# Layer 0 of a four-layer network: steps of 32 queries and all keys, head mixing on sixteen 32x32 tiles, transposes and key sums on VectorE

## The chip, the cores and the metric

The kernel runs on one NeuronCore of a Trainium2 chip. The metric is device time in microseconds (us) of one execution; less is better. The engines named below are TensorE (PE; its weight loads are listed as PEld), VectorE (DVE), ScalarE (ACT), GpSimd (POOL) and SyncE (SP), which issues most DMAs. SBUF is the on-chip memory of 128 partitions; PSUM takes TensorE's results, in eight banks of 512 float32 numbers per partition.

## What is computed

All data is float32. The input x is (4, 512, 32, 32): 4 images of 512 channels and 1024 positions ("tokens"). Each of four layers reads x normalized over groups of 16 channels and adds its result to x. The change is in layer 0, an attention whose 8 heads of 64 channels are mixed before the softmax, and whose probabilities are normalized over each whole map:

```python
q = jnp.einsum('oc,bct->bot', w_q, xf).reshape(b, heads, hd, t)   # k, v alike
attn = jnp.einsum('bhdq,bhdT->bhqT', q, k) * scale
attn = jnp.einsum('gh,bhqT->bgqT', w_head, attn)       # head mixing
attn = jax.nn.softmax(attn, axis=-1)
mean = jnp.mean(attn, axis=(-2, -1), keepdims=True)
var = jnp.var(attn, axis=(-2, -1), keepdims=True)
attn = (attn - mean) / jnp.sqrt(var + EPS)
attn = attn * in_gamma[None, :, None, None] + in_beta[None, :, None, None]
out = jnp.einsum('bhqT,bhdT->bhqd', attn, v)
out = out.reshape(b, t, c)
out = out @ w_proj.T + b_proj
```

Since the softmax's rows sum to 1, the map's mean is 1/1024; its variance needs the sum of squares of the probabilities. Layer 1 is a small simulated circuit that yields one factor per channel, layer 2 an ordinary attention, layer 3 a read of the 8 best of 2048 memory rows per token.

## The kernel before

Everything is in `fast_net`. Channels lie on partitions (`KC` = 4 chunks of 128). Layer 0 goes image by image. The projections q, k (`project`, matmuls at L159), v (`project_tokens`, L172) and the output p (`put_out`) each take 64 matmul instructions of 512 columns; a float32 matmul is recorded as two instructions.

The attention of one image is cut into 32 units `UNITS0` of 128 queries (block `j`) by 256 keys (part `c`).

- `scores` (L343): 8 matmuls with 64 rows (one head's channels) by 128 columns (queries), for the 8 heads, into two PSUM tiles. DVE (L351) and ACT (L353) copy them to `ss`. Eight DMAs of 128 KB on SP (L357) put the rows into `s2`, so that the 8 heads of 16 queries lie on the 128 partitions.
- `mix` (L374): one matmul per 16 queries x 128 keys, with the data as the stationary operand and the 128x128 matrix `wmix` (scale times `w_head`, block by block) as the moving one. The result has keys on partitions; ACT takes the exponential (L378) into `places`, and its square (L390). DVE sums the exponentials over the parts of 128 keys (L397), POOL sums the squares (L402).
- `apply` (L416): v times the exponentials, `pv` of 64x128 per head, two heads side by side in the column halves of the array. After the last part of a block, `finish` sums the remaining 128 partitions with matmuls against ones (L438); ACT copies, DVE inverts (L449) and scales `pv` into `o` (L466), POOL squares the scale (L450, L451). Rows of the inverse go to `seen`, by which the program checks at its end that the range of float32 held.

`pin` keeps an engine's instructions in the order in which they are written, so PE's order is that of the loop: `scores` of a unit, `mix` of the unit two before, `apply` of the one three before. `prepare` (the next image's statistics on DVE, L274, and normalization on DVE, L287) and `gating` (layer 1 of the image before) are generators that give a piece per unit. At the end of an image come q of the next image, the last units, k, `instance_norm` (the scale and shift of `o` on DVE, L498), v, the first two units of scores, and p. The `circuit` constants (DVE, POOL) come after the first image's v. SP's queue holds, in order, the `ss` to `s2` copies, the weights (`load_w`, L200, two buffers, each queued after the projection that frees its place) and the next image's x. POOL's queue holds additions and the DMAs of `put_out` (L511, L515).

Layers 2 and 3 come after layer 0 has ended for all images. In layer 2 the output rows pass through three buffers `xr` (L832 load, L833 ACT, L835 DVE, L836 store).

Of the kernel before, what the change touches and what calls it, by code (L numbers as in the profile page):

```python
# [40 lines left out]
def fast_net(ctx: ExitStack, tc: tile.TileContext, a: dict, out: bass.AP, flag: bass.AP):  # L41
# [7 lines left out]
    ps_s = stage.enter_context(tc.tile_pool(name="ps_s", bufs=2, space=PSUM))  # L49
    ps_t = stage.enter_context(tc.tile_pool(name="ps_t", bufs=2, space=PSUM))  # L50
    ps_m = stage.enter_context(tc.tile_pool(name="ps_m", bufs=2, space=PSUM))
# [5 lines left out]
    def mm_tile(name):  # L57
        return ps_m.tile([P, NB], F32, tag="mm", name=name)

    def small_ps(name):  # L60
        return ps_t.tile([P, NB], F32, tag="tp", name=name)
# [22 lines left out]
    for i in range(P // NH):  # L84
# [21 lines left out]
    )  # L106


    NQ16 = P // NH
    wmix = const.tile([P, NH, NQ16], F32, tag="wmix", name="wmix")  # L110
    nc.gpsimd.memset(wmix, SCALE)
    nc.gpsimd.affine_select(
        out=wmix, in_=wmix, compare_op=ALU.is_ge, fill=0.0, base=0,
        pattern=[[0, NH], [-NH, NQ16]], channel_multiplier=1,
    )
    nc.gpsimd.affine_select(
        out=wmix, in_=wmix, compare_op=ALU.is_ge, fill=0.0, base=NH - 1,
        pattern=[[0, NH], [NH, NQ16]], channel_multiplier=-1,
    )

    seen = const.tile([P, NB], F32, tag="seen", name="seen")
# [31 lines left out]
    def project(w, src, name, evacuate, chunks=range(KC)):  # L153

        for m in chunks:
            ps = ps_s.tile([P, T], F32, tag="sc", name=f"{name}_{m}")
            for n in range(T // NB):
                for k in range(KC):
                    pin(nc.tensor.matmul(  # L159
                        ps[:, n * NB:(n + 1) * NB],  # L160
                        w[:, k, m * P:(m + 1) * P], src[:, k, n * NB:(n + 1) * NB],
                        start=(k == 0), stop=(k == KC - 1),
                    ))
            evacuate(m, ps)

    def project_tokens(w, src, name, evacuate):

        for t in range(0, TC, 2):
            ps = ps_s.tile([P, 2, C], F32, tag="sc", name=f"{name}_{t}")
            for i in range(2):  # L170
# [11 lines left out]
    TB = 2 * P  # L182
    UNITS0 = [(j, c) for j in range(TC) for c in range(T // TB)]
    vs_row = [dram.tile([1, C], F32, tag=f"vs_{b}", name=f"vs_{b}") for b in range(B)]

# [1574 lines left out]
```

## Time and profile before

| | us |
|---|---|
| median of 3 runs (3045.35 to 3047.05) | 3046.58 |
| the profiled execution | 3045.97 |
| its span, first to last instruction | 3044.2 |
| PE busy | 2938.4 |
| DVE busy | 1694.3 |
| POOL busy | 1379.2 |
| ACT busy | 1153.2 |
| layer 0's mixing matmuls (`mx`, L374) | 499.6 |
| layer 0's scores (`sc`, L343) | 259.1 |
| layer 0's values (`pv`, L416) | 251.8 |
| layer 0 to 2 border, by the last p of layer 0 | 1641 |

Layer 0 takes the first 1641 us of the span, layer 2 up to about 2568, layer 3 the rest. The page tells the clock granted to TensorE as `PEclk`. In a group's row stand the line, the engine, the operation, what it writes and reads with the shape (rows*columns of the array for matmuls), the count, the busy us and mean ns of one, and the idle time before it. Busy is the union of the group's intervals; since matmuls are pipelined, busy divided by the count is the pace, and the mean is longer. In the order of time a line has start, length, engine, line and what it is.

### The profile page before, as it was taken

To read this page: it belongs to the slowest core of one execution; us is meant where nothing else is said; L and a number is where in the kernel's file an instruction comes from. 1 tells how busy PE (TensorE), PEld (TensorE's weight loads), DVE (VectorE), ACT (ScalarE), POOL (GpSimd) and SP (SyncE) were. 2 spreads that over 40 slices of the span, in tenths; PEclk is the share of its full clock that TensorE was granted. 3 is DMA by queue.
4 is the path that set the end of the run, shared out by engine and by line. 5 is a ranking of instruction groups with operands and counts; after the bars stand their busy time and mean duration, and the time that the engine had idled before them with its cause. 6 is when DMAs were issued, how large, how long until landed. Compare 5 with 4: busy or idle time off the path is not lost.

```text
span 3044.2 us, 41932 instructions
## 1 busy us (share of the span) xinstructions
PE 2938.4 (97%) x16102; PEld 1681.0 (55%) x16102; DVE 1694.3 (56%) x1588; ACT 1153.2 (38%) x1480; POOL 1379.2 (45%) x1147
## 2 busy tenths in 40 slices
PE   7799999999999999999999999999999999999995
PEld 3488855888558885588853334334334334444442
DVE  1377823778237782368633452461471444878876
ACT  0266612666126661266612421530440351221211
POOL 2066622666226661266612630650460362665664
PEclk9899999999999999999999999999999999999997
DMA  2345405554055440554423002101200203676665
GB/s 80 110 129 137 126 28 147 150 135 126 28 151 151 129 126 28 151 154 129 123 87 111 1 14 93 32 1 69 71 1 28 97 1 107 181 216 207 190 187 146
DMA packets 238696, 318.03 MB, mean 104 GB/s; under 512 B 34701, under 2 KB 198541, under 8 KB 234010
## 3 DMA queue, kind: packets, MB, share of 16 engines
q1 hardware_dynamic: 207368, 231.05, 26.2%
q0 software_dynamic: 29696, 84.18, 9.2%
q8 instruction: 130, 2.13, 0.3%
q14 instruction: 76, 0.62, 0.1%
q10 hardware_dynamic: 1426, 0.05, 0.0%
HBM read 155.52 MB, written 25.17 MB: 59 GB/s over the span
## 4 chain that ended last, share of the span: by engine, by line
PE 87%; DVE 4%; POOL 3%; issue 3%; DMA 1%; ACT 1%; SPq 0%; DVEq 0%; ACTq 0%; POOLq 0%
PE mx L374 15%; PE at L879 14%; PE pv L416 8%; PE p L159 7%; PE k L159 7%; PE sc L343 7%; PE v L172 7%; PE q L159 7%; PE sc_c L760 5%; PE pv_c L792 5%; PE sum L438 2%; POOL ep_c L776 1%; PE rs_c L811 1%; DVE es_c L777 1%; ACT places L768 1%
## 5 line engine op out<-in xcount | busy, mean ns | idle before, releaser
L397 DVE TENSOR_REDUCE places<-places 128x1024 f32<-128x3072 f32 (+1 forms) x128 | 429.0, 3352 | 284.3 <-ACT places L378 282.8
L402 POOL TENSOR_TENSOR es<-es,e 128x1024 f32<-128x1024 f32 x192 | 455.2, 2371 | 228.2 <-ACT e L390 220.0
L374 PE MATMUL mx<-wmix,s 128*128 128x128 f32 x4096 | 499.6, 280 | 1.4 <-ACT places L378 1.1
L374 PEld LDWEIGHTS mx<-wmix,s 128*128 128x128 f32 x4096 | 475.0, 191 | 45.0 <-issue 41.3
L879 PE MATMUL at<-memT,xn_d 128*128 128x512 f32 x1024 | 445.0, 592 | 0.0
L896 POOL DMA_INDIRECT got<-in_mem,ix x256 | 278.2, 1087 | 211.1 <-issue 110.4
L768 ACT ACTIVATE places<-sc_c 128x1024 f32<-128x1024 f32 x256 | 248.2, 1021 | 315.8 <-PE sc_c L760 296.0
L378 ACT ACTIVATE places<-mx 128x512 f32<-128x512 f32 x512 | 305.7, 597 | 158.9 <-PE mx L374 151.3
L879 PEld LDWEIGHTS at<-memT,xn_d 128*128 128x128 f32 x1024 | 192.1, 190 | 230.9 <-issue 230.6
L776 POOL TENSOR_TENSOR ep_c<-places 128x1024 f32<-128x1024 f32 x96 | 234.9, 2448 | 155.5 <-ACT places L768 149.4
L343 PE MATMUL sc<-k,q 64*128 64x256 f32 x2048 | 259.1, 392 | 18.2 <-DVE ss L351 15.2
L777 DVE TENSOR_TENSOR es_c<-es_c,ep_c 128x1024 f32<-128x1024 f32 x96 | 151.9, 1582 | 212.2 <-POOL ep_c L776 212.0
L760 PE MATMUL sc_c<-q,k 64*128 64x512 f32 x1024 | 257.4, 621 | 5.3 <-ACT places L768 3.7
L390 ACT ACTIVATE e<-places 128x1024 f32<-128x1024 f32 x256 | 255.6, 1048 | 1.0 <-POOL es L402 1.0
L416 PE MATMUL pv<-places,v 128*64 128x128 f32 x4096 | 251.8, 276 | 0.0
L792 PE MATMUL pv_c<-places,v 128*64 128x512 f32 x1024 | 249.2, 607 | 2.0 <-ACT places L768 2.0
L353 ACT COPY ss<-sc 128x1024 f32<-128x1024 f32 x128 | 129.5, 1012 | 289.9 <-PE sc L343 269.5
L416 PEld LDWEIGHTS pv<-places,v 128*64 128x64 f32 x4096 | 220.9, 137 | 18.0 <-issue 3.0
L343 PEld LDWEIGHTS sc<-k,q 64*128 64x128 f32 x2048 | 188.6, 188 | 76.5 <-issue 36.5
L351 DVE COPY ss<-sc 128x1024 f32<-128x1024 f32 x128 | 156.0, 1220 | 48.0 <-PE sc L343 31.2
L760 PEld LDWEIGHTS sc_c<-q,k 64*128 64x128 f32 x1024 | 88.9, 187 | 156.4 <-issue 129.5
L402 POOL TENSOR_TENSOR es<-e,e 128x1024 f32<-128x1024 f32 x32 | 75.4, 2355 | 218.7 <-ACT e L390 218.7
(227 smaller groups left out, 3151.1 us busy)
## 6 DMA issues: line engine op xcount, KB each, us to landing
s<-ss SPq DMA_DIRECT2D x1024, 128.0 KB
xn<-in_x SPq DMA_DIRECT2D x16, 512.0 KB
xr<-in_x POOLq DMA_DIRECT2D x32, 256.0 KB, 3.3
x<-xr POOLq DMA_DIRECT2D x32, 256.0 KB, 2.5
xn_c<-x SPq DMA_DIRECT2D x16, 512.0 KB
xr_c<-x SPq DMA_DIRECT2D x32, 256.0 KB
x<-xr_c SPq DMA_DIRECT2D x32, 256.0 KB
xn_d<-x SPq DMA_DIRECT2D x16, 512.0 KB
```

Of the source, the lines that this page charges most:

```text
L159: pin(nc.tensor.matmul(ps[:, n * NB:(n + 1) * NB], w[:, k, m * P:(m + 1) * P], src[:, k, n * NB:(n + 1) * NB], start=(k == 0), stop=(k == ...
L343: pin(nc.tensor.matmul(sc[:, r, m, :], q[r * HD:(r + 1) * HD, 2 * i + m, j * P:(j + 1) * P], k_[r * HD:(r + 1) * HD, 2 * i + m, c * TB:(c ...
L374: pin(nc.tensor.matmul(mx[:, i], s2[:, half * (NB // P) + i, t * P:(t + 1) * P], wmix, start=True, stop=True,))
L378: pin(nc.scalar.activation(e[:, :, half * (NB // P):(half + 1) * (NB // P), :], mx.rearrange("p i g q -> p g i q"), AF.Exp,))
L397: pin(nc.vector.tensor_reduce(es, places[:, at + (c == 0):at + 3].rearrange("p t g q -> p g q t"), AX.X, ALU.add))
L402: pin(nc.gpsimd.tensor_add(es2, e2s[0] if (c, t) == (0, 1) else es2, e2))
L416: pin(nc.tensor.matmul(pv[r * HD:(r + 1) * HD, gp, :], I["v"][:, tt, g * HD:(g + 1) * HD], ev[:, g, :], start=(tt == 0 and gp == 0), stop= ...
L760: pin(nc.tensor.matmul(sc[:, r, :], I["k"][r * HD:(r + 1) * HD, m, t * P:(t + 1) * P], I["q"][r * HD:(r + 1) * HD, m, n * NB:(n + 1) * NB] ...
L768: nc.scalar.activation(e, sc, AF.Exp)
L792: pin(nc.tensor.matmul(pv[r * HD:(r + 1) * HD, :], I["v"][:, t, h * HD:(h + 1) * HD], e[:, r, :], start=(t == 0), stop=(t == TC - 1),))
L879: pin(nc.tensor.matmul(sc[:, n * NB:(n + 1) * NB], xn3[b][:, k, tt * P:(tt + 1) * P], memT[k][:, i0:i0 + NB], start=(k == 0), stop=(k == K ...
L896: pin(nc.gpsimd.indirect_dma_start(out=got[:, i, :], out_offset=None, in_=a["mem"], in_offset=bass.IndirectOffsetOnAxis(ap=ix[:, i:i + 1], ...
```

## The change

Layer 0's attention goes in 32 steps per image of 32 queries and all 1024 keys.

- Scores: for each half of the keys, 8 heads' matmuls of 64 rows x 32 columns, moving 512 keys each, into one pair of banks `sc`; ACT copies both halves. Sixteen DMAs of 64 KB put 8 heads x 4 queries on each quarter of 32 partitions of `s2`.
- `mix`: `wmix` (32 x 32) is now the stationary operand, for 16 tiles of the array: row group r holds 8 queries (2 x 4), column group t takes a quarter of the keys. The result has head and query on partitions; ACT takes the exponentials, 1024 per instruction, into `e`.
- `reduce`: DVE's `bn_stats` (eight of 256 elements a step) gives mean and squared deviations, from which the sums over keys of the exponentials and of their squares follow; two DVE transposes of 32x32 blocks put keys back on partitions, into `eT`.
- `apply` runs seven steps behind, two key parts a step. `sums` adds the parts with one matmul of 32 columns per 128 queries; the inverse goes through DRAM (`r_rows`) and comes back spread (`rb`), by DMAs on POOL's queue. `scale` (DVE) writes blocks of `o` to DRAM (`o_rows`), and `collect` reads them back.
- The projections are fills in the steps: v in steps 0 and 1, p of the image before in steps 2 to 5, the next q in steps 32 to 35, k after the last step. All layer 0 PSUM tiles are fixed (`sc`, `pt`, `mx0`, `mx1`).
- `prepare`'s normalization and `instance_norm`'s scaling move from DVE to POOL, the `vs` DMAs from SP to POOL. The circuit comes before the first k. Weights share three buffers with `ss` (`ws`), and the output buffers `xr` are two in layers 0 and 2. Layers 2 and 3 take their other buffers from `e` and `eT`; layer 2 loads its weights in one place (`load2`).

```diff
-    ps_s = stage.enter_context(tc.tile_pool(name="ps_s", bufs=2, space=PSUM))
-    ps_t = stage.enter_context(tc.tile_pool(name="ps_t", bufs=2, space=PSUM))
-    ps_m = stage.enter_context(tc.tile_pool(name="ps_m", bufs=2, space=PSUM))
+    ps_a = stage.enter_context(tc.tile_pool(name="ps_a", bufs=1, space=PSUM))
+    mx = ps_a.tile([P, 4, NB], F32, tag="mx", name="mx")
+    pairs = {at: ps_a.tile([P, 2, NB], F32, tag=at, name=at) for at in ("sc", "pt")}
+    pairs.update(mx0=mx[:, 0:2], mx1=mx[:, 2:4])
...
+    NS = 32
...
+    o_rows = [dram.tile([P, TC, NB], F32, tag=f"o_{b}", name=f"o_{b}") for b in range(B)]
+    r_rows = [dram.tile([NS, NS], F32, tag=f"r_{i}", name=f"r_{i}") for i in range(2)]
...
+    STEPS = T // NS
+    LAG = 7
+    NK = T // 4
...
+    e = apool.tile([P, 2, 2, 2, NK], F32, tag="e", name="e")
+    eT = apool.tile([P, 2, TC, NS, NS], F32, tag="eT", name="eT")
+    eT_flat = eT.rearrange("p a b k x -> p (a b k x)")
+    o_full = eT_flat[:, 2 * KC * T:3 * KC * T]
+    wp_full = eT_flat[:, 3 * KC * T:3 * KC * T + KC * C].rearrange("p (k c) -> p k c", k=KC)
...
+        w = apool.tile([P, KC, C], F32, tag="ws", bufs=3, name=name)
...
+            pin(nc.gpsimd.tensor_scalar(
...
+    def take_k(b, m, at):
+        I = img[b]
+        if m == 0:
+            I["k"] = big("k", f"k0_{b}")
+        project(I["w_k"], tokens(I["xn"]), m, at,
+                lambda ps: pin(nc.vector.tensor_copy(
+                    I["k"][:, m, :].rearrange("p (t b j) -> p t j b", t=4, j=NS),
+                    ps.rearrange("p (t j b) -> p t j b", t=4, j=NS))))
...
+        project_tokens(I["w_v"], lambda k, t: I["xn"][:, k, t::TC], i, at,
+                       lambda ps: pin(nc.scalar.copy(I["v"][:, 2 * i:2 * i + 2, :], ps)))
...
+    def sum_v(b):
...
+        pin(nc.vector.tensor_scalar_mul(row, vps[0:1, :], float(T)))
+        nc.gpsimd.dma_start(out=vs_row[b], in_=row)
...
+    def scores(b, s, n):
+        I = img[b]
...
+        if n == 0:
+            I["ss", s] = apool.tile([P, 2, T], F32, tag="ws", bufs=3, name=f"ss_{b}_{s}")
+        ss = I["ss", s]
+        sc = pairs["sc"]
+        for m in range(KC):
+            for r in range(2):
+                pin(nc.tensor.matmul(
+                    sc[m * NS:(m + 1) * NS, r, :],
+                    q[r * HD:(r + 1) * HD, m, s * NS:(s + 1) * NS],
+                    k_[r * HD:(r + 1) * HD, m, n * NB:(n + 1) * NB],
+                    start=True, stop=True,
...
+        pin(nc.scalar.copy(ss[:, :, n * NB:(n + 1) * NB], sc))
+        if n == 0:
+            return
+        s2 = I["s2", s] = apool.tile([P, 2, T], F32, tag="s2", bufs=2, name=f"s2_{b}_{s}")
+        del I["ss", s]
+        for m in range(KC):
+            for r in range(2):
+                for qq in range(2):
+                    at = m * NS + qq * (NS // 2)
+                    nc.sync.dma_start(
+                        out=s2[r * KC + m::NH, qq], in_=ss[at:at + NS // 2, r, :])
+    def mix(b, s):
+        s2 = img[b].pop(("s2", s))
+        for t in range(4):
+            for r in range(4):
+                pin(nc.tensor.matmul(
+                    mx[t * NS:(t + 1) * NS, r, :].rearrange("p (qq k) -> p qq k", qq=2),
+                    wmix[r * NS:(r + 1) * NS], s2[r * NS:(r + 1) * NS, :, t * NK:(t + 1) * NK],
+                    start=True, stop=True,
...
+    def exps(s, half):
+        pin(nc.scalar.activation(
+            e[:, half].rearrange("p r qq k -> p (r qq k)"), flat2(pairs[f"mx{half}"]), AF.Exp))
+    def reduce(b, s, half):
+        I = img[b]
+        j, i = divmod(s, 4)
+        if s % 4 == 0 and half == 0:
+            I["st", j] = apool.tile([P, 4, 4, 2, 6], F32, tag="st", bufs=2, name=f"st_{b}_{j}")
+        st = I["st", j]
+        for r in range(2):
+            for qq in range(2):
+                pin(nc.vector.bn_stats(st[:, i, 2 * half + r, qq, :], e[:, half, r, qq, :]))
+        pin(nc.vector.transpose(
+            eT[:, j % 2].rearrange("p b (qq i r) x -> p i r qq b x", qq=2, i=4)[
+                :, i, 2 * half:2 * half + 2],
+            e[:, half].rearrange("p r qq (b x) -> p r qq b x", x=NS),
+        ))
+    def apply(b, s):
...
+                        eT[:, j % 2, t, :, 4 * g:4 * g + 4],
...
+        s_ = small.tile([P, 2, 4, 4], F32, tag="sums", name=f"sums_{nm}")
+        order = "p qq i r -> p i r qq"
+        pin(nc.gpsimd.tensor_add(s_.rearrange(order), st[:, :, :, :, 1], st[:, :, :, :, 4]))
+        yield
+        ps = small_ps(f"sum_{nm}")[:, 0:NS]
+        pin(nc.tensor.matmul(
+            ps, same, s_.rearrange("p qq i r -> p (qq i r)"), start=True, stop=True))
+        ri = small.tile([P, NS], F32, tag="ri", name=f"ri_{nm}")
+        pin(nc.vector.reciprocal(ri, ps))
...
+        rows = r_rows[j % 2]
+        pin(nc.gpsimd.dma_start(out=rows, in_=ri[0:NS]))
+        pin(nc.gpsimd.tensor_scalar(ok[:, 0], ri, R_LO, None, ALU.is_ge))
+        pin(nc.gpsimd.tensor_scalar(ok[:, 1], ri, R_HI, None, ALU.is_le))
+        for i in range(2):
+            pin(nc.gpsimd.tensor_add(seen0, seen0, ok[:, i]))
+        rb = I["rb", j] = apool.tile([P, KC, P], F32, tag="rb", bufs=2, name=f"rb_{nm}")
+        for r in range(2):
+            pin(nc.gpsimd.dma_start(
+                out=rb[r * HD:(r + 1) * HD],
+                in_=rows.rearrange("(gp r x) y -> r gp (x y)", r=2, x=4)[r].partition_broadcast(HD),
+            ))
...
+    def scale(b, j):
+        I = img[b]
+        rb = I.pop(("rb", j)).rearrange("p gp (q qq x) -> p qq gp x q", q=4, qq=2)
+        pv = pairs["pt"][:, 0, :].rearrange("p (gp qq x q) -> p qq gp x q", gp=KC, qq=2, q=4)
+        o = apool.tile([P, KC, NH, NS // 2], F32, tag="o2", bufs=2, name=f"o_{b}_{j}")
+        o_v = o.rearrange("p kc (gp r) x -> p r gp x kc", r=2)
+        for r in range(2):
+            h = slice(r * HD, (r + 1) * HD)
+            for par in range(2):
+                pin(nc.vector.tensor_mul(
+                    o_v[par * HD:(par + 1) * HD, r], pv[h, par], rb[h, par]))
+        nc.sync.dma_start(
+            out=o_rows[b][:, j, :], in_=o.rearrange("p kc g x -> p (kc g x)"))
+    def collect(b):
+        nc.sync.dma_start(
+            out=o_full.rearrange("p (j x) -> p j x", j=TC), in_=o_rows[b])
+        nc.sync.dma_start(out=wp_full, in_=a["w_proj"])
...
+        o = o_full.rearrange("p (jk g x) -> p g jk x", g=NH, x=NS // 2)
...
+            pin(nc.gpsimd.tensor_scalar(
+                o[:, g], o[:, g], al[:, g:g + 1], bb[:, g:g + 1], ALU.mult, ALU.add))
...
+    def put_out(b, m, at):
...
-                xr = apool.tile([P, NB], F32, tag="xr", bufs=3, name=f"xr_{b}_{m}_{n}")
+                xr = apool.tile([P, NB], F32, tag="xr", bufs=2, name=f"xr_{b}_{m}_{n}")
...
+        project(wp_full, lambda k, n: o[:, k, 4 * n:4 * n + 4], m, at, add_out)
...
-                xr = apool.tile([P, NB], F32, tag="xr", bufs=3, name=f"xr_c{b}_{m}_{n}")
+                xr = apool.tile([P, NB], F32, tag="xr", bufs=2, name=f"xr_c{b}_{m}_{n}")
...
     first()
-    take_k(0)
-    take_v(0)
     circuit()
...
+    for m, at in enumerate(("mx1", "sc", "pt", "mx0")):
+        take_k(0, m, at)
...
+    def step(b, s, fill=(), between=lambda: None):
+        fill = dict(fill)
+        def put(where):
+            for take, at in fill.get(where, ()):
+                take(at)
+        if s < STEPS:
+            scores(b, s, 0)
+        between()
+        put(0)
+        old = s - 2
+        j, part = divmod(s - LAG, 4)
+        if 0 <= old < STEPS:
+            mix(b, old)
+            exps(old, 0)
+        if 0 <= j < TC and part == 0:
+            next(img[b]["tail"])
+        if s < STEPS:
+            scores(b, s, 1)
+        if 0 <= old < STEPS:
+            exps(old, 1)
+        put(1)
+        if j > 0 and part == 0:
+            scale(b, j - 1)
+        if 0 <= j < TC:
+            apply(b, s - LAG)
+        if part == 3 and 0 <= j + 1 < TC:
+            img[b]["tail"] = sums(b, j + 1)
+            next(img[b]["tail"])
+        if 0 <= old < STEPS:
+            reduce(b, old, 0)
+            reduce(b, old, 1)
...
-        for s, u in enumerate(UNITS0):
-            if s >= 2:
-                scores(b, u)
-                mix(b, UNITS0[s - 2])
-            if s >= 3:
-                apply(b, UNITS0[s - 3])
-            if s >= 4:
-                next(behind, None)
-            if s >= 11:
...
+        vs = chunks(take_v, b)
+        ps = chunks(lambda b, m, at: put_out(b, m, at), b - 1) if b > 0 else []
+        for s in range(STEPS):
+            if s == STEPS - 1:
+                nxt = img[0 if last else b + 1]
+                keys = ("Wq", "Wk", "Wv") if last else ("w_q", "w_k", "w_v")
+                nxt[keys[0]] = load_w(keys[0], f"{keys[0]}n_{b}")
+            fill = {}
+            if s < 2:
+                fill = {0: [(vs[2 * s], ("pt", "mx1")[s])], 1: [(vs[2 * s + 1], ("mx0", "pt")[s])]}
+            elif s < 6 and b > 0:
+                fill = {1: [(ps[s - 2], "pt")]}
+            def between():
+                if s >= 8 and (s - LAG) % 4:
+                    next(behind, None)
+                if s >= 12 and (s - LAG) % 4:
+                    next(ahead, None)
+            step(b, s, fill, between)
+            if s == 1:
+                sum_v(b)
         run_out(ahead)
-        (take_q2 if last else take_q)(0 if last else b + 1)
-        mix(b, UNITS0[-2])
-        apply(b, UNITS0[-3])
-        mix(b, UNITS0[-1])
-        apply(b, UNITS0[-2])
-        (take_k2 if last else take_k)(0 if last else b + 1)
-        apply(b, UNITS0[-1])
-        later(len(waiting))
+        nxt[keys[1]] = load_w(keys[1], f"{keys[1]}n_{b}")
+        qs = chunks(take_q2, 0) if last else chunks(take_q, b + 1)
+        ks = chunks(take_k2, 0) if last else chunks(take_k, b + 1)
+        for s, fill in zip(range(STEPS, STEPS + LAG), (
+            {1: [(qs[0], "sc")]}, {1: [(qs[1], "sc")]}, {1: [(qs[2], "mx0")]}, {1: [(qs[3], "mx1")]},
+            {}, {}, {},
+        )):
+            step(b, s, fill)
+            if s == STEPS + 3:
+                nxt[keys[2]] = load_w(keys[2], f"{keys[2]}n_{b}")
+        scale(b, TC - 1)
+        collect(b)
+        for m, at in enumerate(("sc", "mx0", "mx1", "sc")):
+            ks[m](at)
         instance_norm(b)
         if last:
-            bv2 = apool.tile([P, C], F32, tag="t1", name="bv2")
+            bv2 = apool.tile([P, C], F32, tag="o2", bufs=2, name="bv2")
             nc.sync.dma_start(out=bv2, in_=a["bv"].partition_broadcast(P))
-            take_v2(0)
-        else:
-            take_v(b + 1)
-            for u in UNITS0[:2]:
-                scores(b + 1, u)
-        put_out(b)
+            for i, at in enumerate(("mx0", "mx1", "sc", "mx0")):
+                take_v2(0, i, at)
+            for m, at in enumerate(("mx1", "sc", "mx0", "mx1")):
+                put_out(b, m, at)
```

## The prediction

> **What bounds the kernel now.** I read the page's busy shares first, then the stretches of layer 0, then one unit of it in order of time. The page:
>
> ```profile
> PE 2938.4 (97%) x16102; PEld 1681.0 (55%) x16102; DVE 1694.3 (56%) x1588; ACT 1153.2 (38%) x1480; POOL 1379.2 (45%) x1147
> PEclk9899999999999999999999999999999999999997
> ```
>
> TensorE (PE) is busy for 97% of the span at full clock, so the time is the sum of its work, stage by stage. The stretches of one image's attention and of the projections that follow:
>
> ```profile
> 152.00:372.00 220.00, 220.00 (x2228) 191.06 (x2228) 171.15 (x110) 151.83 (x205) 136.44 (x77) 1.00 0.49 131
> 372.00:526.00 154.00, 152.56 (x658) 82.22 (x658) 53.62 (x66) 34.15 (x44) 35.46 (x33) 1.00 0.29 87
> ```
>
> The columns are length, then busy us of PE, PEld, DVE, ACT, POOL, then clock, DMA share, GB/s. In the attention PE has no idle time, DVE is at 78%, the DMA engines at 49%. One unit (128 queries x 256 keys), and three rows that tell when tiles of the array run side by side:
>
> ```profile
> 303.97 2.00 PE L343 MATMUL sc<-k,q 64*128 64x256 f32 x16
> 305.90 3.90 PE L374 MATMUL mx<-wmix,s 128*128 128x128 f32 x32
> 309.73 1.97 PE L416 MATMUL pv<-places,v 128*64 128x128 f32 x32
> ...
> 108.76 3.59 PE L317 MATMUL vs<-w_v,ybar 128*1 128x512 f32 x8
> ...
> 302.16 1.03 PE L438 MATMUL sum<-places,ones 128*64 128x512 f32 x4
> ...
> 376.35 27.66 PE q L159 x64
> 755.48 27.66 PE q L159 x64
> ```
>
> The reader should see four things. Head mixing is half of a unit (3.9 of 7.8 us). A matmul is recorded as two instructions; on the whole array one of 512 columns takes 27.66 / 64 = 0.432 us, and the single column tile of `vs` 3.59 / 8 = 0.449: a small tile alone is no faster. Two tiles in different halves are: `sum` 1.03 / 4 = 0.26, `sc` 2.00 / 16 = 0.125 for 256 columns where one alone would take 0.216. And the period from one image's q projection to the next is 379.1 us.
>
> **The change, engine by engine, for a step of 32 queries x 1024 keys** (as many pairs as a unit, so 32 steps per image where there were 32 units).
>
> *PE, scores.* 16 matmuls (32 instructions) of 512 columns on eight 64x32 tiles, in two halves. Eight at once give 2 passes x 0.43 = 0.86 us a half. `sc` shows what a group pays on entry: 2.00 - 8 x 0.216 = 0.27. So 1.15 a half, 2.3 a step (now 2.0). If only pairs run together, as the trace shows, it is 32 x 0.257 = 8.2.
>
> *PE, mixing.* 32 instructions on sixteen 32x32 tiles. All at once: 0.86 + 0.27, with some issue time 1.3 us; pairs only: 8.2; four at a time: 32 x 0.432 / 4 + 0.3 = 3.8. I take 1.3: both kinds of pair in the trace (two row halves, two column halves) reach the full factor of two, and nothing shows a limit at two. The Trainium skill, TensorE: Matmul & The Clock Gate, Part 3 (packing small matmuls), states 10.6 times for sixteen tiles and starts 4 ns apart; with two passes of 592 ns that is an estimate of 1.3 us. No row here shows more than two tiles.
>
> *PE, the rest.* Values stay at 1.97 a step. The `sum` matmuls (32.9 + 32.9 us) go; a 32-column one per 128 queries takes their place, below 0.3 us. PE per step: 2.3 + 1.3 + 2.0 = 5.6 us, with the small one 5.7.
>
> *DVE.* It loses the key reductions (429 us), the score copies (156) and the 512-wide reciprocals (107). It gains eight statistics of 256 elements and two transposes of 1024 a step. The rows:
>
> ```profile
> 23.74 1.28 DVE L221 BATCH_NORM_STATS2 st_a<-xn 128x6 f32<-128x512 f32 x2
> ...
> L351 DVE COPY ss<-sc 128x1024 f32<-128x1024 f32 x128 | 156.0, 1220 | 48.0 <-PE sc L343 31.2 <-DMA s<-ss 13.7 <-issue 2.1
> L724 DVE TENSOR_SCALAR xn_c<-xn_c,sa,ta 128x1024 f32<-128x1024 f32 x16 | 50.3, 3143 | 0.0
> L227 DVE TENSOR_SCALAR xn<-xn,gm_a,grstd_a 128x1024 f32<-128x1024 f32 x4 | 3.3, 814 | 6.6 <-POOL grstd_a L125 6.6
> ```
>
> Statistics of 512 follow each other at 0.60 us; at 1.04 ns an element 256 take 0.335, eight 2.7 us. No transpose is in the trace. Its ends are 0.81 and 3.14 us (the fastest and slowest 1024-element rows); I take the copy's 1.2, since it too reads and writes each element once. So 2.7 + 2.4, and per 128 queries four scalings (0.42 each) and a short reciprocal, 0.5 a step: 5.6 us, as long as PE. Ends 4.8 and 9.5.
>
> *ACT.* Two score copies and two exponentials of 1024, 1.01 to 1.05 each: 4.1 us a step, hidden. The squares (256 us) go.
>
> *SP and DMA.* 16 copies of 64 KB a step where there were 8 of 128 KB, the same megabyte.
>
> ```profile
> L357 SPq DMA_DIRECT2D s<-ss x1024: 532/599/2220, 116.8 to 1512.9; - x171
> L323 SPq DMA_DIRECT2D vs<-vrow x4: 244/252/317, 113.1 to 1236.8; - x4
> L836 SPq DMA_DIRECT2D x<-xr_c x32: 319/320/320, 1884.6 to 2569.6; - x32
> ```
>
> The present copy goes from 128 rows to 16 x 8 pieces and costs 0.6 us to issue; copies of plain rows cost 0.25 (one row) to 0.32 (128 rows). The new ones go from 16 rows to 16 rows; I take 0.31 plus 0.045 between two: 5.7 us a step, hidden only just. At 0.64 it is 10.3. Moving the bytes: 131 GB/s at a share of 0.49 makes 4 us a megabyte, hidden. The mixing comes two steps after the scores: 2T - 3.7 us are left for 5.7 of issue and 2.5 to 3.3 of landing (the page's landings of x and xr), so T below 6.0 would wait here. The skill speaks against this edit: DMA: Bandwidth & Descriptors, Bandwidth, has 0.95 us for a copy of 64 KB and advises 1 MiB; sixteen in a row would make 15 us a step and a kernel of about 3770 us (estimates). In the trace a copy is issued every 0.64 us while the one before is still in flight, so I do not add them up.
>
> *POOL.* 530 us of additions go. The last norm's 8 scalings (1.3 each by the 512-element rows), the next image's 4 normalisations (2.4 by the 1024-element rows), the vs row's copies and about 20 small operations with 3 DMAs per 128 queries (6 us) come. A read-back DMA waits for its write to land, 2.5 us, with gating's small operations behind it; they have a step each. The norm's 15 us lie beside the k and v projections (55 us).
>
> *Waits.* One PSUM pair holds the scores: half 1 starts after ACT's copy of half 0 (1.0), under the mixing; the next step starts after the copy of half 1, under the values. Once per 128 queries the values wait for the scaling, which is queued on DVE behind the last step's statistics and transposes: about 2 us every 4 steps beside PE's slack, 0.4 a step. Step time T = 5.7 + 0.4 = 6.1 us, in which PE, DVE and SP are all within 0.5 of each other.
>
> **The sum.** One image now, PE's path: v in steps 0 and 1: 27.7 + 2 x 2.3 + 3.6 (`vs`) = 35.9. Steps 2 to 5 with the last image's output projection: 27.7 + 4 x 3.6 = 42.1. Steps 6 to 31: 26 x 6.1 = 158.6, and 5 for the next image's statistics on DVE. Steps 32 to 35 with q: 27.7 + 2.6 + 8 = 38.3. Three value steps: 7. k, its last copy, the norm's small matmul: 29.7. Together 316.6, against 379.1.
>
> First image: k ends at about 84 us, the circuit's DVE work (113 to 129.6 in the trace, with TensorE waiting from 117 to 131) now lying under q and k. 84 + 35.9 + 24.4 + 163.6 + 38.3 + 7 + 29.7 = 383; three more make 1333. The same point, layer 2's k done, is now at 1580.3: 247 less. The last v and output projections take 57.4 for 61 before: 4 less. Layer 2: the output buffers `xr` are two, not three; their cycle (store 2.5, load 2.6, ACT 1.6, DVE 1.3) is 8 us a pair where PE makes one in 6.9; PE's three PSUM pairs cover part: 3 us an image, 12 in all (0 to 30). Layer 3 is PE's as before. Span 3044.2 - 251 + 12 = 2805; the profiled execution took 1.8 us more than its span, and the median is 0.6 above it: 2807 us.
>
> **Rivals.**
> - *Fewer tiles at once* (slower). Four at a time: scores 4.0, mixing 3.8, T = 9.8; an image costs 3.4 + 17 + 96 + 5 = 121 more, the kernel about 3290; pairs only, over 4000. For: the trace shows two. Against: no sign of a limit. It turns slower where T passes 8.3 (239 / 108 steps = 2.2 more).
> - *DVE bounds.* A transpose of 2.4 us makes T 8.0: +1.9 x 108 = 3012; of 3.14, T = 9.5: 3174. For: the same operation has 0.81 and 3.14 us rows. Against: copies and reductions hold about 1.1 ns an element.
> - *SP's issue bounds.* At 0.64 each T is 10.3: 3260. Against: only the split pattern costs that.
> - *All overlaps hold.* T = 5.1 to 5.6, mixing 1.1: 2690 to 2750.
>
> **How the numbers follow.** Main case 0.60 (2700 to 2900 alone); better than 2700 0.04; DVE, SP or the copies bound at T of 7 to 8.3 (2900 to 3040) 0.11; beyond that (3050 to 3260) 0.09; fewer tiles 0.16 (3290 and up). A measurement of this kernel can tell about 0.2% from no change. Faster 0.75, same 0.02, slower 0.23. The range 2700 to 3200 leaves out 0.2.
>
> **What would show it.** The `mx` group under 200 us in all with 16 tiles starting within 0.2 us; `sc` near 290; DVE transposes near 1.2 us each; SP's copies near 0.3; q projections 317 us apart; no PE idle before the first scores. A `mx` of 4 us a step, a transpose above 2.4, or PE waiting at `mx` for a DMA would prove the forecast wrong.

## The result, and the profile after

The changed kernel takes 3360.1 us (median of 4 runs, 3358.1 to 3363.9); the kernel before took 3046.3 us beside it (4 runs). The ratio is 1.103, with a 95% interval of 1.101 to 1.105: 10% slower, where 2807 us had been forecast. Lines of the page, of the profiled execution (span 3362.2 us):

```profile
PE 2788.4 (83%) x17966; PEld 1191.0 (35%) x17966; DVE 1619.3 (48%) x2511; ACT 959.0 (29%) x1031; POOL 998.6 (30%) x1421
PEclk9877789877799778898788999999999999999997
...
PE 50%; SPq 28%; DVE 6%; issue 5%; DMA 5%; POOL 3%; ACT 2%; ACTq 0%; DVEq 0%; POOLq 0%
SPq L377 28%; PE at L927 12%; PE mx L167 5%; PE sc L167 4%; PE pv_c L838 4%; PE sc_c L806 4%; PE p L167 2%; PE k L167 2%; PE q L167 2%; PE v L179 2%; PE mx L179 2%; POOL e L822 2%; PE pt L420 2%; PE pt L179 2%; PE pt L167 1%
```

Before, TensorE was busy for 97% of the span at full clock. Now it is at 83%, and in layer 0, the first 23 of the 40 slices, the clock that it is granted is 0.7 to 0.9 (the records of the granted clock in this trace hold two values, 1.0 and 0.5, and 0.5 for 641 us). No engine is full. The chain of work that ended last names what is: 28% of the span is `SPq L377`, the issue of the copies from `ss` to `s2` on SP's queue. The instructions that write or read these tiles, with the shortest, median and longest duration in ns and the first and last start in us:

```profile
L384 PE MATMUL mx<-s,wmix x4096: 584/1028/1058, 124.0 to 1830.3; 32*32 32x512 f32 x196
L377 SPq DMA_DIRECT2D s<-ss x2048: 492/587/1975, 95.7 to 1827.2; - x187
```

and the waits of TensorE, in us, how often, and the longest:

```profile
PE mx L384 <- DMA s<-ss: 320.5, 86, 11.1
PE mx L384 <- DMA o<-o: 54.6, 12, 6.1
PE pt L420 <- DVE o L487: 29.9, 25, 3.7
```

A copy holds SP's queue for 0.587 us and the next starts 0.045 us later. Sixteen of them are 10.1 us, and the starts of the mixing of neighbouring steps lie 11.16 us apart (mean over the mixings in steps 7 to 31 of the four images). A step in order of time (start, length, engine, line, then in brackets how long the engine had been idle and what ended it):

```profile
1295.63 24.68 SPq L377 DMA_DIRECT2D s<-ss  x36
1295.92 1.29 PE L384 MATMUL mx<-s,wmix 32*32 32x512 f32 x32 [3.41 <-DMA s<-ss]
...
1302.78 1.36 DVE L404 BATCH_NORM_STATS2 st<-e 128x6 f32<-128x256 f32 x4
1304.06 1.23 DVE L405 STREAM_TRANSPOSE eT<-e 128x1024 f32<-128x1024 f32 x1
1307.17 0.32 PEld L384 LDWEIGHTS mx<-s,wmix 32*32 32x32 f32 x32 [5.50 <-issue]
1307.20 2.02 PE L384 MATMUL mx<-s,wmix 32*32 32x512 f32 x32 [4.62 <-DMA s<-ss]
```

SP issues 36 copies without a break, TensorE has waited 4.62 us when the mixing starts, and VectorE has had nothing to do since 1305.3. The two mixings also show the clock: the same 32 instructions take 1.29 us (1.15 at full clock) and, after the longer wait, 2.02.

Where the 318 us of span came from: layer 0 ended with layer 2's first scores at 1963.2, before at 1642.4, 320.8 later; layer 2 and layer 3 together changed by -3. The q projections of the four images are 440.9, 457.4 and 451.1 us apart, before 361.3, 379.1 and 379.1.

### The profile page after: what moved, and what is told of

The parts are those of the page before. It is cut to its first block, busy times and chain, and to the rows that moved or that the text cites. A ratio compares the mean times of both kernels' runs of the same rounds, so it can differ in the third digit from the quotient of the medians.

```text
span 3362.2 us, 46319 instructions
## 1 busy us (share of the span) xinstructions
PE 2788.4 (83%) x17966; PEld 1191.0 (35%) x17966; DVE 1619.3 (48%) x2511; ACT 959.0 (29%) x1031; POOL 998.6 (30%) x1421
## 4 chain that ended last, share of the span: by engine, by line
PE 50%; SPq 28%; DVE 6%; issue 5%; DMA 5%; POOL 3%; ACT 2%; ACTq 0%; DVEq 0%; POOLq 0%
SPq L377 28%; PE at L927 12%; PE mx L167 5%; PE sc L167 4%; PE pv_c L838 4%; PE sc_c L806 4%; PE p L167 2%; PE k L167 2%; PE q L167 2%; PE v L179 2%; PE mx L179 2%; POOL e L822 2%; PE pt L420 2%; PE pt L179 2%; PE pt L167 1%
## 5 line engine op out<-in xcount | busy, mean ns | idle before, releaser
L404 DVE BATCH_NORM_STATS2 st<-e 128x6 f32<-128x256 f32 x1024 | 354.9, 409 | 432.2 <-ACT e L391 428.8
L384 PE MATMUL mx<-s,wmix 32*32 32x512 f32 x4096 | 209.6, 846 | 407.9 <-DMA s<-ss 320.5
L391 ACT ACTIVATE e<-mx 128x1024 f32<-128x1024 f32 x256 | 262.1, 1027 | 571.9 <-PE mx L384 498.1
L362 PE MATMUL sc<-k,q 64*32 64x512 f32 x4096 | 355.9, 753 | 21.1 <-ACT ss L368 19.4
L814 ACT ACTIVATE eT<-sc_c 128x1024 f32<-128x1024 f32 x256 | 248.2, 1021 | 379.8 <-PE sc_c L806 373.9
L420 PEld LDWEIGHTS pt<-eT,v 128*64 128x64 f32 x4096 | 271.7, 160 | 186.5 <-issue 117.6
L405 DVE STREAM_TRANSPOSE eT<-e 128x1024 f32<-128x1024 f32 x256 | 314.6, 1229 | 35.0 <-PE pt L420 35.0
L420 PE MATMUL pt<-eT,v 128*64 128x128 f32 x4096 | 301.9, 311 | 29.9 <-DVE o L487 29.9
L822 POOL TENSOR_TENSOR e<-eT 128x1024 f32<-128x1024 f32 x96 | 231.8, 2418 | 156.6 <-ACT eT L814 138.6
L838 PE MATMUL pv_c<-eT,v 128*64 128x512 f32 x1024 | 250.5, 610 | 2.3 <-ACT eT L814 2.3
```

The lines of the kernel that those rows point to most:

```text
L362: pin(nc.tensor.matmul(sc[m * NS:(m + 1) * NS, r, :], q[r * HD:(r + 1) * HD, m, s * NS:(s + 1) * NS], k_[r * HD:(r + 1) * HD, m, n * NB:(n ...
L391: pin(nc.scalar.activation(e[:, half].rearrange("p r qq k -> p (r qq k)"), flat2(pairs[f"mx{half}"]), AF.Exp))
L404: pin(nc.vector.bn_stats(st[:, i, 2 * half + r, qq, :], e[:, half, r, qq, :]))
L405: pin(nc.vector.transpose(eT[:, j % 2].rearrange("p b (qq i r) x -> p i r qq b x", qq=2, i=4)[:, i, 2 * half:2 * half + 2], e[:, half].rea ...
L420: pin(nc.tensor.matmul(pv[r * HD:(r + 1) * HD, gp, :], I["v"][:, t, g * HD:(g + 1) * HD], eT[:, j % 2, t, :, 4 * g:4 * g + 4], start=(t == ...
L822: nc.gpsimd.tensor_add(two, es[0], es[1])
```

## The experiments

In all of them the step is the mean distance just described. A kernel that was run once has one time; the kernel before took 3044.6 to 3044.9 us beside these runs.

### Which property of a copy costs the 0.59 us

A kernel of copies alone, without the network's computation, in forms that differ in one thing each:

```diff
+    for m, r, qq in cuts:                      # d_st: the source in DRAM
+        nc.sync.dma_start(out=d_st[r * KC + m::NH, qq], in_=d_src[at:at + 16, r, :])
...
+    for m in range(KC):                        # k_st: both halves of a source partition
+        for qq in range(2):
+            nc.sync.dma_start(out=k_st[m::KC, qq], in_=src[at:at + 16])
```

> A kernel that does nothing of the computation: it copies the input to the output and otherwise issues copies of nine forms, each into a tile of its own, so that the time of one issue on its queue can be read. In the changed kernel one copy of 16 rows of 4 KB from SBUF to SBUF, landing on every eighth partition, held SP's queue for 0.587 us, while 128 rows between DRAM and SBUF held it for 0.32. Theory 1 (both ends in SBUF cost the time): every form with both ends in SBUF takes 0.55 to 0.65 us whatever its rows (16 strided rows, 16 rows that lie together, 32 rows, 128 rows of 1 KB, short rows of 1 KB, and 32 strided rows from 16 source partitions), and the same 16 rows to or from DRAM take 0.30 to 0.35. Theory 2 (the landing pattern costs it): the strided forms take 0.59, from DRAM too, and the 16 rows that lie together 0.32. Theory 3 (the time goes with the rows): 16 rows 0.59, 32 rows about 1.2, 128 rows more. On the ACT queue the same strided copies should take what they take on SP.

The instructions that read `src` and `d_src` (shortest, median and longest ns; first and last start). `a_st` is the copy of the changed kernel, `b_st` has 16 partitions that lie together, `c_dram` writes to DRAM, `d_st` reads from it, `e_st` is 128 rows of 1 KB, `f_st` 32 rows of 4 KB, `g_st` 128 rows of 512 bytes to 16 partitions, `h_st` 16 rows of 1 KB, `k_st` 32 rows of 4 KB from 16 partitions; `i_st` and `j_st` are `a_st` on ACT's and POOL's queue:

```profile
L41 ACTq DMA_DIRECT2D i_st<-src x16: 500/501/1283, 8.6 to 79.6; - x16
L41 POOL DMA_DIRECT2D j_st<-src x16: 481/483/613, 8.9 to 22.1; - x16
L54 SPq DMA_DIRECT2D c_dram<-src x16: 302/430/1658, 68.2 to 88.1; - x16
L83 SPq DMA_DIRECT2D h_st<-src x16: 587/587/596, 114.2 to 123.7; - x16
L63 SPq DMA_DIRECT2D e_st<-src x8: 587/599/601, 98.5 to 103.0; - x8
L70 SPq DMA_DIRECT2D f_st<-src x8: 512/590/598, 103.7 to 108.4; - x8
L76 SPq DMA_DIRECT2D g_st<-src x8: 591/596/605, 109.1 to 113.6; - x8
L90 SPq DMA_DIRECT2D k_st<-src x8: 590/606/705, 124.3 to 129.0; - x8
```

```profile
L59 SPq DMA_DIRECT2D d_st<-d_src x16: 497/587/588, 88.5 to 97.9; - x16
```

(`a_st` and `b_st` ran while the other two queues were issuing, their issues reached 2.7 us, and they say less.) Sixteen rows or 128, 16 KB or 128 KB, strided or not: 0.587 to 0.606. Theories 2 and 3 fall. Theory 1 holds for the seven forms on SP with both ends in SBUF. It fails at `d_st`, which comes from DRAM and still costs 0.587, and `c_dram`, for which it had 0.30 to 0.35, took 0.43. The same strided copies cost ACT 0.50 and POOL 0.48, not what they cost SP. The single records tell what else matters. The first copy of `d_st` took 0.497, and in the changed kernel a copy that comes after a pause takes 0.49; those that follow one another take 0.587. So a copy that lands in SBUF costs SP 0.632 us from start to start when it stands in a row. Copies in a row to DRAM took 0.417 where nothing disturbed them. Why loads of 128 rows from DRAM that stand alone take 0.32 in the large kernels while a lone copy of 16 rows takes 0.49 was not settled.

### The same bytes in half the copies

```diff
-            for r in range(2):
-                for qq in range(2):
-                    at = m * NS + qq * (NS // 2)
-                    nc.sync.dma_start(
-                        out=s2[r * KC + m::NH, qq], in_=ss[at:at + NS // 2, r, :])
+            for qq in range(2):
+                at = m * NS + qq * (NS // 2)
+                nc.sync.dma_start(out=s2[m::KC, qq], in_=ss[at:at + NS // 2])
```

> Eight copies of 128 KB a step instead of sixteen of 64 KB: the two halves of a source partition go in one copy, to 32 partitions. Same bytes, same rows of 4 KB. Theory 1 (SP pays by the copy, and SP bounds the step): SP needs 8 x 0.634 = 5.1 us a step, it is no longer the bound, and the step falls from 10.9 us to what TensorE and VectorE take, 6.1 to 7.0: 4 x 30 x (3.9 to 4.8) = 470 to 575 us less, 2785 to 2890 us. Rival (SP pays by the row): 8 x 1.2 = 9.6 us or more, 3250 to 3370 us. Rival (the transfers themselves set the step, not their issue: the 16 DMA engines are 0.58 busy at 4 KB rows of 0.344 us): no change, 3330 to 3370 us.

2884.1 us (4 runs, 2880.6 to 2891.1), 0.947 of the kernel before, interval 0.945 to 0.948: 476 us under the changed kernel by merging two copies into one, and faster than both kernels. The step is 6.74 us. Page, copies and waits of this kernel:

```profile
PE 2627.7 (91%) x17966; PEld 1146.6 (40%) x17966; DVE 1614.2 (56%) x2511; ACT 956.4 (33%) x1031; POOL 997.3 (35%) x1421
...
PEclk9999999999999999999999999999999999999997
```

```profile
L376 SPq DMA_DIRECT2D s<-ss x1024: 542/598/1832, 95.7 to 1355.4; - x171
```

```profile
PE pt L418 <- DVE o L485: 56.5, 25, 3.7
PE mx L382 <- DMA s<-ss: 37.3, 36, 1.9
```

A copy of twice the size costs the same 0.6 us; half as many leave SP 5.1 us of a step. TensorE's wait for copies falls from 320 to 37 us, and the clock is at 0.9 or more in every slice but the last. Both rivals fall: SP does not pay by the row, and the transfers did not set the step of 11.2, since the bytes are the same.

### Twelve copies

```diff
+                if m < 2:
+                    nc.sync.dma_start(out=s2[m::KC, qq], in_=ss[at:at + NS // 2])
+                    continue
```

> Twelve copies a step: four of 128 KB (the halves of the source partition in one) and eight of 64 KB, with the same bytes. Theory (SP pays 0.632 us for every copy in a row, whatever its size, and SP sets the step of the changed kernel but not that of the run with eight copies): 12 x 0.632 = 7.6 us, and the 0.8 that the step of the changed kernel has above 16 x 0.632 = 10.1, so 8.4 us; 4 x 30 x 2.5 = 300 us less than the changed kernel, 3060 us, between 3010 and 3090. Rival (the step goes with the number of copies all the way from sixteen to eight): the middle of 3360 and 2884, 3100 to 3140 us.

3097 us, a little above the theory's range and just below the rival's. The step tells more than the total: its median is 8.40 us where 8.4 had been worked out, its mean 8.74, since a few steps take 15. From sixteen copies (median 11.04) to twelve it falls by 2.64, or 0.66 a copy, beside 0.632 as the price of one. That is near the theory's slope; its total was 37 us short. By the means the step falls by 2.42, 0.61 a copy, and from twelve copies to eight by 2.00, 0.50 a copy, so this run alone hardly tells the theory from its rival. That SP has room at eight copies is told by the waits of the kernel of eight wide copies: 37 us for copies where there were 320.

### Copies on other queues

Eight of the sixteen narrow copies on ACT's queue:

```diff
-                    nc.sync.dma_start(
+                    (nc.sync, nc.scalar)[qq].dma_start(
```

> The sixteen copies unchanged, eight of them issued from ACT's queue and eight from SP's. Theory 1 (the issue bounds): SP has 8 x 0.634 = 5.1 us a step, ACT its two copies and two exponentials, 2 x 1.01 + 2 x 1.03 = 4.1, and 8 x 0.634 = 5.1 more, 9.2 us; ACT bounds, the step is 9.2 to 9.7 and the time 4 x 30 x (1.2 to 1.7) = 145 to 205 us less, 3155 to 3215 us. Rival (the transfers set the step): 3330 to 3370 us.

and five:

```diff
-                    nc.sync.dma_start(
+                    (nc.scalar if 4 * m + 2 * r + qq in (2, 5, 8, 11, 14) else nc.sync).dma_start(
```

> As the run with eight, but five copies on ACT's queue and eleven on SP's. Theory 1: SP 11 x 0.634 = 7.0 us a step, ACT 4.1 + 5 x 0.634 = 7.3; the step is 7.3 to 7.9 us and the time 4 x 30 x (3.0 to 3.6) = 360 to 430 us less, 2930 to 3000 us, so that three copies fewer on ACT give some 220 us over the run with eight. Rival (the transfers set the step): 3330 to 3370 us in both. Rival (TensorE, which runs at half its clock in much of layer 0 and is busy 0.65 to 0.74 of it, cannot follow): a step of at least 0.7 x 10.9 = 7.6 us at the clock as it is, 3000 us or more.

3490 us with eight on ACT, slower than the changed kernel; 3188 with five. Steps of 12.18 and 9.48 us where 9.2 to 9.7 and 7.3 to 7.9 had been worked out. Neither theory predicted this. The order of time with eight shows what the sum over ACT had left out:

```profile
257.46 1.01 ACT L368 COPY ss<-sc 128x1024 f32<-128x1024 f32 x1 [0.53 <-PE sc L362]
...
258.50 5.26 ACTq L377 DMA_DIRECT2D s<-ss  x8
...
263.81 1.02 ACT L391 ACTIVATE e<-mx 128x1024 f32<-128x1024 f32 x1 [5.34 <-DMA s<-ss]
...
264.88 1.15 PE L384 MATMUL mx<-s,wmix 32*32 32x512 f32 x32 [3.54 <-ACT e L391]
```

The eight issues stand between the score copy and the second exponential. The next mixing needs the PSUM banks that this exponential reads, so the 5.26 us lie in a loop of mixing, exponential, copy, and not beside it. The 32 instructions of a mixing, which stand in this loop, take 2.02 us in the median there (1.15 at full clock), so the half clock may have a share in its length; no run took that apart. TensorE no longer waits for copies at all, it waits for ACT:

```profile
PE mx L384 <- ACT e L391: 493.4, 118, 7.3
PE pt L420 <- DVE o L487: 35.5, 25, 3.7
```

With five, TensorE waits 151 us for copies and 118 for ACT. (The 455 and 1079 us in the next expectation count the waits of the weight loads too; those of the matmuls are 118 and 493.) To see whether the place was all, the five were moved behind the exponential:

```diff
             exps(old, 1)
+        if s < STEPS:
+            copies(b, *img[b].pop("late"), 1)
```

> As the run with five copies on ACT's queue, but these five are issued after the step's second exponential instead of between the score copy and that exponential. Theory (in the two ACT runs the issues stood in the chain exponential - mix - exponential, TensorE waited 455 and 1079 us for the second exponential, and the room for the copies was there otherwise): SP 7.0 us, ACT 7.3, a step of 7.3 to 8.2 us, 2930 to 3040 us. Rival (ACT pays more than 0.63 us for an issue in other ways, or the landing of the copies is late): 3150 to 3200 us as before.

3151 us, a step of 9.13: 0.35 less than with five in the first place, and 37 us. So the place was a part, the smaller one, and the time lies in the rival's range. TensorE waits above all for copies again:

```profile
PE mx L391 <- DMA s<-ss: 181.6, 65, 5.8
```

The trace shows a part of the rest. The landing of a copy is told by a semaphore, a counter; the copies name eight of them in turn, on whichever queue they are issued, and each waits for the counter that it names. Behind the first copy of each step, 397 of SP's copies name a semaphore that a copy of ACT's had used just before. They took 152 us more than 0.632 each, and 133 of these passed before ACT's copy had landed. All of SP's copies behind the first of a step took 243 us more than 0.632 each. That is 1.9 us a step; with it SP's 11 x 0.632 = 7.0 comes to 8.9 of the 9.13. What makes the rest stays open.

At last eight on POOL's queue instead of ACT's:

```diff
-                    nc.sync.dma_start(
+                    (nc.sync, nc.gpsimd)[qq].dma_start(
```

> The sixteen copies of 64 KB unchanged, eight issued from SP's queue and eight from POOL's. Theory (only the issue bounds, and POOL's queue has room): SP 8 x 0.632 = 5.1 us a step; POOL 8 x 0.48 = 3.9 (its copies in the kernel of copies took 0.483) beside 1.5 to 2 us of its own work; neither bounds, and the time is near that of eight wide copies, 2870 to 2950 us. Rival (POOL's queue is in order: its copies wait for ss, and the sums, the reciprocals' round trip and the next image's normalising stand behind them): values wait for rb, 3000 to 3200 us. Rival (the transfers set the step): 3330 to 3370 us.

3055 us, a step of 8.00 (POOL's copy 0.483, SP's 0.588). The rival's range has it, but its reason, values that wait for `rb`, does not show: the values wait 37 us for the scaled blocks `o`, where they waited 57 in the kernel of eight wide copies. In the first steps of images 1 to 3, where POOL also loads and stores the rows of the output projection, the first five distances take 65 us together where they take 51 in the kernel of eight wide copies; this is 42 us over three images. TensorE waits for copies for 106 us, there 37. That POOL's queue, in order, is what delays them fits, but was not shown by a run of its own.

With the same sixteen transfers the step falls to 9.5, 9.1 and 8.0 us in three of the four, and in the fourth TensorE's wait for copies is gone and one for ACT has come: the transfers did not set the step of 11.2, the issue on SP did. None of the four does what was hoped for. On ACT the copies stood ahead of work that TensorE waits for, and shared semaphores delayed SP's own; for POOL the like is likely but not shown.

### The half clock

Products without use ahead of the mixing, to keep TensorE busy while it waits:

```diff
+        for i in range(7):
+            pin(nc.tensor.matmul(
+                mx[:, i % 4, :], ones, img[b]["k"][:, i % 4, 0:NB], start=True, stop=True))
```

> The changed kernel with seven products more per step (128x128 by 128x512, of the ones by k, written where the mix writes after them), put ahead of the mix, where TensorE waits for the copies; they keep it busy for 7 x 0.59 = 4.1 us a step at the full clock. Theory (SP sets the step, the half clock in the waits only follows from them): the granted clock in layer 0 rises from 0.77 to 0.86 to 0.95 or more, and the time stays within 3330 to 3380 us. Rival (TensorE at half its clock is part of what sets the step): a time 50 to 200 us shorter, 3160 to 3310 us. Rival (TensorE has no room for it): over 3400 us.

3552 us, in the range of the rival that TensorE has no room for them, so it tells nothing of what the half clock costs. A product took 0.86 us, two passes of 0.43, and I had counted 0.59, the latency of one pass. Seven were 6.0 us, and TensorE itself set a step that has a median of 11.3. With three, the range in the same line set to 3:

> The changed kernel with three products more per step ahead of the mix instead of seven. In the run with seven each took TensorE 2 x 0.43 = 0.86 us at the full clock, not the 0.59 that its size was taken from, so that seven were 6.0 us and TensorE itself set a step of 11.3; three are 2.6 us, and TensorE's work is 5.4 + 2.6 = 8.0 us of a step of 11.0. Theory (SP sets the step, the half clock follows from the waits): the clock in layer 0 rises, and the time stays within 3340 to 3380 us. Rival (the half clock is part of what sets the step): 50 to 200 us shorter, 3160 to 3310 us. If the clock stays where it was and TensorE's work at half of it (16 us) sets the step: over 3600 us.

3388 us, 8 above the theory's range. The same stretch of the first image, in the changed kernel and in this one (length, then busy us of PE, PEld, DVE, ACT, POOL, granted clock, DMA share, GB/s):

```profile
130.00:430.00 300.00, 186.28 (x2496) 74.32 (x2496) 158.62 (x316) 108.06 (x109) 50.58 (x112) 0.74 0.64 113
```

```profile
130.00:430.00 300.00, 228.07 (x2648) 95.26 (x2646) 157.77 (x316) 106.55 (x109) 50.43 (x112) 0.93 0.64 113
```

The clock goes from 0.74 to 0.93, and VectorE, ACT, POOL and the bytes in this stretch are the same as before within 2%: the step is 11.07 for 11.16. The 28 us that it is slower lie in the first steps of images 1 to 3 (60 to 62 us for the first five distances, 52 in the changed kernel), where TensorE has no idle time. TensorE still waits 195 us for copies. So the half clock costs at most about 0.1 us a step here; it follows from the waits. The Trainium skill, TensorE: Matmul & The Clock Gate, Part 1, describes such a gate, which looks at how busy the array has been and halves the clock after an idle window. The rows above agree that filling the waits lifts the clock; the skill's warning would by itself have pointed to a gain from it, and there is none while another queue sets the pace.

### What sets the step once SP does not

The kernel of eight wide copies, with less work for VectorE: four of a step's eight statistics read 32 of their 256 keys, so that this kernel leaves a part of the key sums out.

```diff
-                pin(nc.vector.bn_stats(st[:, i, 2 * half + r, qq, :], e[:, half, r, qq, :]))
+                pin(nc.vector.bn_stats(
+                    st[:, i, 2 * half + r, qq, :], e[:, half, r, qq, 0:NK >> 3 * half]))
```

> The kernel with eight wide copies a step, but the four statistics of the second half of each step read 32 of their 256 keys (this leaves part of the key sums out; nothing else changes). In a stretch of 19 steps of that kernel VectorE was busy 6.05 us of 6.7 a step; each of these four goes from 0.35 to an estimated 0.10 to 0.16 us, 0.8 to 1.0 us a step less. Theory (with SP out of the way VectorE sets the step, as the rival of the prediction had it): the step falls from 6.74 us to 5.9 to 6.1, where TensorE's 5.4 and its waits take over, 4 x 30 x (0.6 to 0.8) = 70 to 100 us less than 2884, 2785 to 2815 us. Rival (TensorE or the copies set the step): 2860 to 2890 us.

2851 us, between the two. One stretch of the first image in the kernel of eight wide copies, and in this one:

```profile
196.00:320.00 124.00, 102.03 (x1758) 49.21 (x1742) 108.53 (x220) 73.28 (x75) 41.04 (x83) 0.94 0.86 176
```

```profile
196.00:320.00 124.00, 102.62 (x1822) 49.94 (x1815) 98.85 (x237) 74.76 (x77) 44.55 (x94) 0.99 0.90 195
```

VectorE goes from 88% to 80%, in steps of 6.74 and 6.43 us: 0.8 us of its work a step less gives 0.31. So VectorE is a part of what sets the step but not all. TensorE is at 82 to 83% in both, and the DMA engines at 86 and 90%. Three resources stand close together there; which of the other two ends last was not taken apart.

## Why the prediction was wrong

**The step that failed** is SP's term: "I take 0.31 plus 0.045 between two: 5.7 us a step, hidden only just", and the reason given against its rival, "only the split pattern costs that". The price was taken from copies that go to or come from DRAM and stand alone in the queue (0.25 to 0.32). The one row for a copy from SBUF to SBUF in a long run was the 0.599 of these very copies, and it was set aside because of its pattern of 16 x 8 pieces. The kernel of copies shows that the pattern has no part in it. With 0.632 the term is 10.1, the step is SP's, and the slack of 2T - 3.7 us, from which the copies were to be hidden, is no help: a queue that is full all the time cannot catch up.

**The rival was right in kind and short in size.** "SP's issue bounds" gave a step of 10.3 and 3260 us. The step is 11.16. What lies above 10.1 can be read from SP's queue. From the first copy of step 7 to that of step 31, 0.6 us a step are issues that took longer than 0.587, 0.3 are pauses between copies and at the step's first, and 0.3 are the other transfers that this queue issues. The longer issues are in the main no wait for an earlier copy: behind the first of each step 140 copies took over 0.1 us more than 0.632, and for 117 of them the copy that had used their semaphore before had landed when the queue came to them. What held these is open. 26 x 4 steps of 5.06 us over the forecast 6.1 make 526 of the 553 us between forecast and result. Its chance was within the 0.09 for 3050 to 3260, and the range ended at 3200, below the 3260 that the prediction itself had worked out for an issue of 0.64.

**The rest of the forecast** can be read where SP is out of the way, in the kernel of eight wide copies, 2884 for 2807:
- Tiles side by side: right. The 32 instructions of a mixing take 1.15 to 1.2 us (forecast 1.3) and `mx` 154.7 us in all (forecast below 200); a half of the scores takes 1.09 (1.15) and `sc` 295.5 us (near 290). The rival of fewer tiles falls.
- VectorE: the transpose takes 1.229 us (1.2), four statistics 1.36 to 1.41 (1.34). With scalings and the next image's statistics VectorE is busy 5.9 us a step, forecast 5.6.
- TensorE: 102.0 us in 18.4 steps, 5.5 a step, forecast 5.7.
- Moving the bytes was forecast at 4 us a megabyte, from 131 GB/s at a share of 0.49. Here 176 GB/s are a share of 0.86, or 205 GB/s at a full share where the old rows made 267. That is 0.86 x 6.74 = 5.8 us a step with the output's and the normalization's transfers: not hidden by much.
- So the step is 6.74 for 6.1, 26 x 4 x 0.64 = 67 of the 77 us.
- Steps 2 to 5 with the output projection take 10.3 to 10.4 us each, once 11.9 (forecast 10.5), and the first scores start at 83 us without the wait for the circuit.
- Layer 2 was to lose 12 us to its two output buffers. From its first scores to its last values it takes 876.9 us after and 880.8 before: it lost nothing.

The view that would have shown all this was named at the end of the prediction: "PE waiting at `mx` for a DMA would prove the forecast wrong". It waits for 320 us there.

## What to carry to other kernels

Price an issue from copies that follow one another in a queue and land where the new ones land, not from lone ones; then multiply by the number of copies, not by their bytes, and compare with the step. If a queue's sum comes near the step, merge copies first: here one access pattern that takes two rows per source partition halved the issues at the same bytes and was worth 476 us, while spreading them over other queues was worth less: 305 us with eight on POOL, at best 209 with five on ACT, and with eight on ACT, ahead of work that others waited for, it cost 130. When TensorE's clock drops together with waits, look for what it waits on before trying to raise the clock.

## What was not expected of the hardware

- Issuing a copy that lands in SBUF costs SP 0.49 us after a pause and 0.587 in a row (0.632 from start to start), for 16 to 128 rows and 16 to 128 KB, from SBUF and from DRAM. Loads of 128 rows from DRAM that stand alone took 0.32. ACT takes 0.50 and 0.60, POOL 0.483. The Trainium skill, DMA: Bandwidth & Descriptors, Bandwidth, advises transfers of 1 MiB; the advice points the right way here. Its 0.95 us for 64 KB, which the page gives for loads from HBM issued by GpSimd and as the time that the DMA engines are busy, is not what a copy cost the queue.
- Rows of 4 KB between SBUF partitions were no faster per byte than rows of 1 KB: in the stretch 196 to 320 us of the kernel of eight wide copies 4746 rows of 4 KB took 1562 us of the DMA engines, 0.329 each, and in the kernel before, from 152 to 372 us, 27770 rows of 1 KB took 1667 us, 0.060 each, or 0.24 for 4 KB.
- With waits of 3 to 5 us in most steps the granted clock stood at 0.74 over 300 us, and at 0.93 when 2.6 us of products without use were put into each.
